# Staging, reads and rows of maxima of a two-layer attention kernel: more room and later issue

## The chip, the cores and the metric

The kernel runs on one core of a Trainium2 chip. The time is that of one execution on the device, in microseconds (us). A core has five engines that run side by side: TensorE (PE; its weight loads are listed as PEld), VectorE (DVE), ScalarE (ACT), GpSimd (POOL) and SyncE (SP), which here does nothing but issue DMAs. Each engine works through its own list of instructions in order; an instruction that waits for a semaphore holds all that stand behind it. A DMA is issued by one of the engines SP, ACT or POOL and is then carried out by 16 DMA engines. Lower times are better.

## The reference

Four sequences of 512 positions with 320 features pass two layers. A layer is self attention, cross attention to a context of 1601 positions with 192 features, and a gated feed-forward step; everything is float32, with 20 heads of 16 features.

```python
def _attn(x, ctx, wq, wk, wv, wo, bo, heads):
    q, k, v = heads_of(x @ wq), heads_of(ctx @ wk), heads_of(ctx @ wv)
    a = softmax(einsum('bhid,bhjd->bhij', q, k) * dh ** -0.5)
    return merge(einsum('bhij,bhjd->bhid', a, v)) @ wo + bo
for each layer:
    h1 = _ln(x, n1_g, n1_b);  x = _attn(h1, h1, q1, k1, v1, o1_w, o1_b, 20) + x
    h2 = _ln(x, n2_g, n2_b);  x = _attn(h2, context, q2, k2, v2, o2_w, o2_b, 20) + x
    h3 = _ln(x, n3_g, n3_b);  a, g = split(h3 @ ff_w1 + ff_b1)
    x = (a * gelu(g)) @ ff_w2 + ff_b2 + x
```

## The kernel before

**Units and chunks.** The work is cut into units. An attention unit is one sequence (b, of 4) and one group of four heads (g, of 5), so a layer has 20 units of self attention, 20 of cross attention and 4 of feed-forward. They are numbered through: layer 0 has units 0 to 19 (self), 20 to 39 (cross), 40 to 43 (feed-forward), layer 1 has 44 to 63, 64 to 83 and 84 to 87. A unit goes over its keys in chunks of 128: four chunks in self attention, 13 in cross attention. For each chunk `main` forms four score tiles (tile `st`, L1165), ScalarE takes their exponential (`pr`, L1175), and a chunk later TensorE multiplies by the values (`av`, L1189).

**High and low parts.** The products take their operands in the type float32r. Queries and keys are therefore split by `split` on GpSimd into a rounded `high` part and the rest, `low`, and a head's parts are stacked on the 32 rows of its slot: the keys as high and low, the queries once as high and low and once the other way round, so that two products sum all four terms. To bring parts to their rows they go through DRAM: writes to `qway` and `kway`, then reads into `q` and `kT`, the tiles that TensorE uses. `move` (L721) records each such group of DMAs in a queue of its unit and `carry` (L666) issues them.

**Maxima first.** The softmax subtracts the maximum of each row before the exponential. So each unit's scores are computed once before, in coarse products (`sps`, L972), and VectorE takes their maxima (`nmax` in self attention, `pm` in cross attention, L989). These products are called pairs; they are handed out by `give` beside the score products of the units before, eight of them in self attention, 26 in cross attention. `max_end` then turns the negative maxima into rows (`turned`, by a transpose on VectorE) and four small DMAs carry them to `nrows`; the third product of each score tile adds them (`st<-nrows,ones`). `max_end` of the next unit is called after the third last chunk of the current one.

**Who sets the order.** All is written out once, in Python, in program order; each engine then runs its part as semaphores allow. A counter `clock["round"]` is raised twice a chunk. Chains of smaller steps (projections `proj` and `early`, `values`, `norm`, `context`, `project`, `divide`) wait with costs and due rounds, and `steps` picks from them once a chunk. At its end it calls `carry`, which goes over the units that have moves left: a move is issued if its buffers are free and at least two rounds have passed since the unit's last move was issued or recorded, up to a budget of three DMAs a call; then come the `errands`, a queue of single tasks with a round each. In this way nearly all DMAs stand on SP's queue in the order in which `carry` met them.

**What the change touches.** `both` (L759) projects queries and keys of a self unit in two halves, into the staging tiles `low` and `high` (L718, one of each); `queries` (L795) does so for cross attention; `keys_of_context` (L823) projects the context's keys into tiles of their own, and its four writes `kway<-stages` and three reads `kT<-kway` follow. `way_free` (L747) says whether a new projection may start. `at_hand` (L1401) says whether a unit's pairs may be handed out: three rounds after its last read was issued. `add_finish` (L1052) divides a finished unit's output by its sums and writes it to `oway`; after the fifth group it adds an errand that reads the sequence's output back into `aT`, and eight `project` steps (L1094) multiply by the output weights. At the start, unit 0 is moved at once by `at_once` (L1405).

Of the kernel before, what the change touches and what calls it, by code (L numbers as in the profile page):

```python
# [9 lines left out]
F32 = mybir.dt.float32  # L10
# [7 lines left out]
B, N, D = 4, 512, 320  # L18
# [5 lines left out]
P = 128  # L24
# [41 lines left out]
def kernel(ctx: ExitStack, tc: tile.TileContext, x, context, ws, out):  # L66
# [57 lines left out]
    nc.vector.memset(fill, 1.0)  # L124


    room = {"turn": 0}

    def take_rooms(l):

# [535 lines left out]
    def carry():  # L666

        room = 3
        for _, what, u in sorted(movers):
            todo = u.moves[what]  # L670
            while todo and todo[0][1]() and clock["round"] >= u.moving[what] + 2 and room > 0:
                room -= todo[0][2]
                todo.popleft()[0]()
            if not todo:
                movers.remove((u.i, what, u))
        while errands and room > 0 and clock["round"] >= errands[0][0] and errands[0][1]():
            errands.popleft()[2]()
# [4 lines left out]
    def split(low, high):  # L682

        nc.gpsimd.tensor_copy(high.bitcast(F32R), low)
        nc.gpsimd.tensor_tensor(low, low, high, ALU.subtract)

    def add_proj(u):
# [28 lines left out]
                add(chain, 0.0, hold, due - 4, yes, lambda: "h" in u.own)  # L716

        def staged():  # L718
            return (one.tile([P, N], F32, tag=n, name=n) for n in ("low", "high"))

        def move(of, n, pairs, may=None):  # L721

            def f():
                if may is None:
                    pending[of] -= 1
                u.moving[of] = clock["round"]
                for i, (to, src) in enumerate(pairs()):
                    queue = (nc.sync, nc.scalar, nc.gpsimd)[i % 3] if start["on"] and u.i == 0 else nc.sync
                    queue.dma_start(out=to, in_=src)  # L729
                if may is not None:  # L730
                    u.open -= 1
                    if not u.open:
                        u.when = -9 if start["on"] else clock["round"]

            if may is None:
                pending[of] += 1
            u.moves[of].append((f, may or yes, n))
            u.moving[of] = clock["round"]
            if (u.i, of, u) not in movers:
                movers.append((u.i, of, u))  # L740
# [5 lines left out]

        def way_free(what):  # L747

            return not pending[what] and (len(users[what]) < 2 or not any(users[what][-2].moves.values()))

        def read_queries(t, keys=None):

# [6 lines left out]
        def both(part):  # L759

            w = N // 2
            at = part * w
            ps = step_bank([P, 512], "qkps")
            for k, _, n in DK:
                nc.tensor.matmul(  # L765
                    ps[:, :w],
                    lhsT=wqk[:n, k, u.g].rearrange("p i d -> p (i d)"),
                    rhs=first.hT[:n, k, at : at + w],
                    start=(k == 0),
                    stop=(k == 2),  # L770
                )
            if part == 0:
                u.stage = tuple(staged())
            low, high = u.stage
            if u.i == 0:
                nc.scalar.activation(high[:, at : at + w].bitcast(F32R), ps[:, :w], AF.Copy, scale=scales[:, 0:1])
                nc.vector.scalar_tensor_tensor(
                    low[:, at : at + w], ps[:, :w], scales[:, 0:1], high[:, at : at + w], ALU.mult, ALU.subtract
                )
            else:  # L780
                nc.scalar.activation(low[:, at : at + w], ps[:, :w], AF.Copy, scale=scales[:, 0:1])  # L781
            if part == 0:
                return
            if u.i:
                split(low, high)
            to_k = on_way("k").rearrange("j h d i n -> j h d (i n)")[:, :, :, :N]
            to_q = on_way("q")
            move("q", 2, lambda: [(to_k[:, 0], high[GD:]), (to_k[:, 1], low[GD:])])
            move("q", 3, lambda: [(to_q[:, e], t[:GD]) for e, t in enumerate((high, low, high))])
            read_queries(to_q, to_k)  # L790
            u.keyed = True
            first.made["q"] += 1
            first.made["k"] += 1
# [242 lines left out]
    def max_end(u):  # L1036

        parts = two.tile([P, SLOT], F32, tag="parts", name="parts")
        high, low = (parts.rearrange("p (j e t) -> p e j t", e=2, t=NQ)[:, e] for e in range(2))
        of = u.nm.rearrange("p (j t) -> p j t", t=NQ)  # L1040
        nc.vector.tensor_copy(high.bitcast(F32R), of)
        nc.vector.tensor_tensor(low, of, high, ALU.subtract)
        turned = two.tile([P, SLOT], F32, tag="turned", name="turned")

        nc.vector.transpose(turned, parts)
        slots = u.rows.bitcast(F32).rearrange("(g s) n -> s g n", s=DH)[0].rearrange("g (t r) -> g t r", t=NQ)
        for i in range(P // SLOT):
            rows = slice(i * SLOT, (i + 1) * SLOT)
            queue = (nc.sync, nc.scalar, nc.gpsimd, nc.sync)[i] if start["on"] else nc.sync
            queue.dma_start(out=slots[:, :, rows], in_=turned[rows, :])  # L1050

    def add_finish(u):  # L1052

        when = [clock["round"]]

        def since(i, n):
            return lambda: len(when) > i and clock["round"] >= when[i] + n

        turned = one.tile([P, N // SLOT, SLOT], F32, tag="oturn", name="oturn")

        def sums():
            nc.vector.transpose(turned.rearrange("p b s -> p (b s)"), u.o)
            u.rd = two.tile([P, N // SLOT], F32, tag="rd", name="rd")
            nc.vector.reciprocal(u.rd, turned[:, :, DH])
            when.append(clock["round"])

        def divide():
            nc.vector.tensor_tensor(  # L1070
                turned[:, :, :DH], turned[:, :, :DH],
                u.rd.rearrange("p (b o) -> p b o", o=1).to_broadcast([P, N // SLOT, DH]), ALU.mult,
            )
            nc.vector.transpose(u.o, turned.rearrange("p b s -> p (b s)"))
            when.append(clock["round"])

        def turn():

            way = o_way[u.b % 2]
            dma(out=way[u.g * HG : (u.g + 1) * HG].rearrange("j s n -> (j s) n"), in_=u.o)  # L1080
            if u.g < G - 1:
                return
            held["written"] += 1

            def read():
                held["read"] += 1
                aT = two.tile([P, 3, N], F32, tag="aT", name="aT")
                for k, at, n in DK:
                    dma(out=aT[:n, k, :], in_=way[at // DH : (at + n) // DH, :DH, :])
                end(aT)  # L1090

            errands.append((clock["round"] + 2, lambda: held["open"] < 2, read))

        def project(aT, t, part):  # L1094
            cols = slice(part * D // 2, (part + 1) * D // 2)
            ps = step_bank([P, 512], "ops")
            for k, at, n in DK:
                for f, m in tiles_of(P):
                    nc.tensor.matmul(  # L1099
                        ps[f : f + m, : D // 2],  # L1100
                        lhsT=aT[:n, k, t * P + f : t * P + f + m],
                        rhs=wo[:n, k, cols],
                        start=(k == 0),
                        stop=(k == 2),
                    )
            nc.vector.tensor_tensor(xs[u.b][:, t, cols], ps[:, : D // 2], xs[u.b][:, t, cols], ALU.add)

        def end(aT):
            now = clock["round"]
            held["open"] += 1  # L1110
            for t in range(NQ):
                for part in range(2):
                    add(
                        "project", (0.317,) * 3, lambda t=t, part=part: project(aT, t, part),
                        now + 6 + u.nch * t + u.nch // 2 * part, yes, lambda: clock["round"] >= now + 3,
                    )
            add("project", 0.0, done, now + 6 + u.nch * NQ)

        def done():
            held["open"] -= 1  # L1120
            after(u)

        r = when[0]
        add("divide", LIGHT, sums, r - 20, yes, since(0, 3))
        add("divide", LIGHT, divide, r - 20, yes, since(1, 1))

        add("divide", 0.0, turn, r - 20, lambda: u.g or held["written"] < held["read"] + 2, since(2, 1))


# [270 lines left out]

    def at_hand(v):  # L1401

        return v.when is not None and clock["round"] >= v.when + 3

    def at_once(v):  # L1405
        chain = "early" if v.early else "proj"
# [157 lines left out]
```

## Time and profile before

| | us |
|---|---|
| median of 3 runs | 3381.98 |
| lowest and highest | 3379.53, 3386.66 |
| profiled execution | 3384.97 |
| its span, first to last instruction | 3383.2 |
| self attention, layer 0 and layer 1 (first score to the next stage) | 443, 397 |
| cross attention, layer 0 and layer 1 | 954, 944 |
| feed-forward, layer 0 and layer 1 | 308, 283 |

The stages are cut at 55, 498, 1452, 1760, 2157 and 3101 us of the span, where the first score product of a stage starts. In a row of the waits stand who waited, for whom, the total in us, the number of waits and the longest one. In a row of the time line stand start, duration, engine (with q for its issuing part), line, operation, tiles, shapes and count, and in brackets the idle time before it and what ended it. In a row by stretches stand, for each engine, busy time and instructions, then the granted clock of TensorE, the share of the 16 DMA engines that was busy, and GB/s.

### The profile page before, as it was taken

The numbers are of one execution on the slowest core, as the hardware profiler recorded it, in microseconds if no ns is written. First come the engines' busy times: TensorE is split into PE (matmuls) and PEld (weight loads), VectorE is DVE, ScalarE is ACT, GpSimd is POOL, SyncE is SP. The second block draws the span as 40 slices with busy tenths as digits, with TensorE's granted clock in tenths as the row PEclk, the third lists the DMA queues.
The fourth block names the chain that finished last, engine by engine and source line by source line (L and its number), as shares of the span: only waits on it lengthen the run. The fifth ranks groups of instructions, "written<-read, shape, count | busy, mean of one in ns | idle before, by whom it ended". The sixth has DMA issues, their size and how long they took to land.

```text
span 3383.2 us, 81116 instructions
## 1 busy us (share of the span) xinstructions
PE 3121.4 (92%) x34290; PEld 1649.8 (49%) x34290; DVE 2096.4 (62%) x2819; ACT 1965.6 (58%) x3909; POOL 1130.3 (33%) x1224
## 2 busy tenths in 40 slices
PE   6889889999989989999999888899999899899999
PEld 3445445445545545445554554454454454454555
DVE  3657776767866876732237777667677677675221
ACT  1555656677767777830116665567677677686110
POOL 2333323443434443410113332234344344343000
PEclk7888999999989999999999999899999899999999
DMA  3343322222222222110023332222222122122000
GB/s 90 107 128 123 104 70 80 82 90 63 74 82 64 89 75 64 50 57 1 18 62 120 117 104 88 83 67 72 72 77 77 51 87 72 51 66 77 8 8 16
DMA packets 209045, 244.14 MB, mean 72 GB/s; under 512 B 60412, under 2 KB 140424, under 8 KB 208680
## 3 DMA queue, kind: packets, MB, share of 16 engines
q1 hardware_dynamic: 207924, 238.02, 22.7%
q8 instruction: 269, 4.41, 0.5%
q14 instruction: 96, 0.79, 0.1%
q10 hardware_dynamic: 308, 0.53, 0.1%
q0 software_dynamic: 448, 0.40, 0.0%
HBM read 130.03 MB, written 107.55 MB: 70 GB/s over the span
## 4 chain that ended last, share of the span: by engine, by line
PE 61%; DMA 17%; DVE 8%; SPq 5%; issue 3%; ACT 3%; POOL 1%; ACTq 0%; POOLq 0%; DVEq 0%
PE st L1165 16%; PE av L1189 13%; PE fps L1295 8%; PE yps L1349 5%; DMA q<-qway 4%; DMA qway<-low 4%; DVE pm L989 4%; DMA qway<-high 3%; PE kps L831 3%; SPq L729 3%; PE sps L972 3%; PE ops L1099 3%; ACT pr L1175 2%; DMA aT<-oway 2%; PE fps L1308 2%
## 5 line engine op out<-in xcount | busy, mean ns | idle before, releaser
L1175 ACT ACTIVATE pr<-st 128x512 f32<-128x512 f32 (+1 forms) x2720 | 1407.0, 602 | 449.5 <-PE st L1165 391.0
L989 DVE TENSOR_REDUCE pm<-sps 128x2 f32<-128x1024 f32 (+1 forms) x975 | 1135.5, 1200 | 228.3 <-PE sps L972 192.7
L1206 POOL TENSOR_TENSOR o<-o,vo 128x512 f32<-128x512 f32 x576 | 741.6, 1288 | 1431.3 <-ACT vo L1205 1412.6
L1165 PE MATMUL st<-q,kT 32*128 32x512 f32 (+1 forms) x5120 | 973.8, 448 | 32.6 <-ACT low L781 16.4
L972 PE MATMUL sps<-kT,q 32*128 32x512 f32 x4800 | 883.2, 453 | 97.8 <-DMA q<-qway 75.2
L1189 PE MATMUL av<-pr,vals 128*32 128x512 f32 (+1 forms) x5440 | 774.4, 638 | 27.4 <-ACT pr L1175 21.3
L1165 PEld LDWEIGHTS st<-q,kT 32*128 32x128 f32 (+1 forms) x5120 | 479.0, 186 | 527.4 <-ACT pr L1175 283.3
L1165 PE MATMUL st<-nrows,ones 32*128 32x512 f32 (+1 forms) x2720 | 646.4, 409 | 40.3 <-DMA nrows<-turned 40.2
L989 DVE TENSOR_REDUCE nmax<-sps 128x2 f32<-128x1024 f32 (+1 forms) x343 | 380.1, 1145 | 232.6 <-PE sps L972 179.7
L972 PEld LDWEIGHTS sps<-kT,q 32*128 32x128 f32 x4800 | 386.9, 192 | 152.8 <-DMA q<-qway 45.7
L1205 ACT COPY vo<-av 128x512 f32<-128x512 f32 x576 | 346.9, 602 | 103.7 <-PE av L1189 96.6
L1165 PEld LDWEIGHTS st<-nrows,ones 32*128 32x128 f32 (+1 forms) x2720 | 335.2, 189 | 79.5 <-DMA nrows<-turned 39.2
L1295 PE MATMUL fps<-hT,w 128*128 128x512 f32 x640 | 284.3, 597 | 0.5 <-DVE hid L1319 0.5
L1318 ACT ACTIVATE gl<-fps,b 128x512 f32<-128x512 f32 x80 | 50.7, 684 | 378.0 <-PE fps L1308 272.1
L1189 PEld LDWEIGHTS av<-pr,vals 128*32 128x32 f32 (+1 forms) x5440 | 112.7, 110 | 294.5 <-ACT pr L1175 274.5
L1319 DVE SCALAR_TENSOR_TENSOR hid<-fps,b,gl 128x512 f32<-128x512 f32 x80 | 56.4, 746 | 265.1 <-ACT gl L1318 265.1
L1295 PEld LDWEIGHTS fps<-hT,w 128*128 128x128 f32 x640 | 118.9, 190 | 148.7 <-issue 144.1
L1349 PE MATMUL yps<-w,hid 128*128 128x320 f32 x640 | 175.9, 434 | 0.4 <-ACT hT L529 0.4
L1099 PE MATMUL ops<-wo,aT 112*32 112x160 f32 (+1 forms) x3072 | 139.1, 320 | 27.7 <-DMA aT<-oway 27.4
L1099 PEld LDWEIGHTS ops<-wo,aT 112*32 112x32 f32 (+1 forms) x3072 | 101.3, 118 | 112.7 <-issue 50.7
L1349 PEld LDWEIGHTS yps<-w,hid 128*128 128x128 f32 x640 | 120.5, 190 | 55.7 <-issue 6.6
L781 ACT ACTIVATE low<-qkps,scales 128x256 f32<-128x256 f32 x78 | 35.3, 473 | 157.4 <-PE qkps L765 70.6
(92 smaller groups left out, 2532.5 us busy)
## 6 DMA issues: line engine op xcount, KB each, us to landing
kway<-stages SPq DMA_DIRECT2D x160, 224.0 KB
q<-qway SPq DMA_DIRECT2D x138, 256.0 KB
kT<-kway SPq DMA_DIRECT2D x80, 384.0 KB
oway<-o SPq DMA_DIRECT2D x80, 256.0 KB
kT<-kway SPq DMA_DIRECT2D x40, 256.0 KB
qway<-high SPq DMA_DIRECT2D x160, 64.0 KB
qway<-high SPq DMA_DIRECT2D x79, 128.0 KB
aT<-oway SPq DMA_DIRECT2D x32, 224.0 KB
```

Source lines behind the costliest of these rows:

```text
L729: queue.dma_start(out=to, in_=src)
L831: nc.tensor.matmul(ps[i * GD : (i + 1) * GD, :w], lhsT=wk_q[rows, k, u.g * GD : (u.g + 1) * GD], rhs=first.kvT[rows, k, i * HALF : i * HAL ...
L972: nc.tensor.matmul(ps, lhsT=u.q[j * SLOT : (j + 1) * SLOT, e, t * P : (t + 1) * P], rhs=u.kT[j * SLOT : (j + 1) * SLOT, u.k0 + s * 512 : u ...
L989: nc.vector.tensor_reduce(to[:, j : j + n], part, AX.X, ALU.max, negate=(ns == 1))
L1099: nc.tensor.matmul(ps[f : f + m, : D // 2], lhsT=aT[:n, k, t * P + f : t * P + f + m], rhs=wo[:n, k, cols], start=(k == 0), stop=(k == 2),)
L1165: nc.tensor.matmul(st[:r, :], lhsT=ones[rows, :r] if e == 2 else u.keys(rows, c), rhs=u.rows[rows, :] if e == 2 else u.q[rows, e, :], star ...
L1175: nc.scalar.activation(p[:r], st[:r], AF.Exp)
L1189: nc.tensor.matmul(ps[j * SLOT : (j + 1) * SLOT, :], lhsT=columns_of[:r, head : head + SLOT], rhs=pr.pop((c, j))[:r, :], start=True, stop= ...
L1205: nc.scalar.copy(vo, ps)
L1206: nc.gpsimd.tensor_tensor(u.o, u.o, vo, ALU.add)
L1295: nc.tensor.matmul(ps, lhsT=w1[:, k, i * FF + c * P : i * FF + (c + 1) * P], rhs=u.hT[:, k, :], start=ahead and k == 0, stop=not ahead and ...
L1349: nc.tensor.matmul(ps[:, :D], lhsT=hid[c][:, t * P : (t + 1) * P], rhs=w2[:, c, :], start=(c == 0), stop=(c == NHC - 1),)
```

## The change

- **Two sets of staging tiles, one output tile.** `low` and `high` come from the pool with two buffers, `aT` from the one with one buffer. `way_free` no longer refuses a projection of queries while writes of an earlier unit are still to be issued; for the context's keys it still does. The output's read now waits until no projection of an earlier output is open.
- **First unit's parts go straight to their rows.** Unit 0 isn't written to DRAM: 24 DMAs, one for each head, half and place, copy 16 rows each from `high` and `low` to `q` and `kT`, on SP, ACT and POOL in turn.
- **Rows of maxima in cross attention are issued a chunk later.** Where a unit and the one before it are both cross attention, the four DMAs of `max_end` become an errand for the next round, put ahead of the other errands; `carry` comes to it after the moves.
- **Reads spaced.** In `carry` a read needs three rounds since the last move, a write still two. Pairs are at hand four rounds after the read instead of three. The output's read comes four rounds after its write instead of two, and its projection five rounds after the read instead of three.

```diff
-            while todo and todo[0][1]() and clock["round"] >= u.moving[what] + 2 and room > 0:
+            while todo and todo[0][1]() and clock["round"] >= u.moving[what] + 3 - todo[0][3] and room > 0:
...
-            return (one.tile([P, N], F32, tag=n, name=n) for n in ("low", "high"))
+            return (two.tile([P, N], F32, tag=n, name=n) for n in ("low", "high"))
...
-            u.moves[of].append((f, may or yes, n))
+            u.moves[of].append((f, may or yes, n, may is None))
...
-            return not pending[what] and (len(users[what]) < 2 or not any(users[what][-2].moves.values()))
+            return not (what == "k" and pending[what]) and (len(users[what]) < 2 or not any(users[what][-2].moves.values()))
...
+            if u.i == 0:
+                for j in range(HG):
+                    for t in range(2):
+                        for h in range(2):
+                            of = (high, low)[h]
+                            slot = slice(j * SLOT + h * DH, j * SLOT + (h + 1) * DH)
+                            away = slice(j * SLOT + (1 - h) * DH, j * SLOT + (2 - h) * DH)
+                            rows = slice(j * DH + t * GD, j * DH + t * GD + DH)
+                            to = [u.kT[slot, u.k0 : u.k0 + N]] if t else [u.q[slot, 0, :], u.q[away, 1, :]]
+                            for x in to:
+                                queue = (nc.sync, nc.scalar, nc.gpsimd)[room["first"] % 3]
+                                room["first"] += 1
+                                queue.dma_start(out=x.bitcast(F32), in_=of[rows, :])
+                u.when = -9
+                u.keyed = True
+                first.made["q"] += 1
+                first.made["k"] += 1
+                return
...
-        for i in range(P // SLOT):
-            rows = slice(i * SLOT, (i + 1) * SLOT)
-            queue = (nc.sync, nc.scalar, nc.gpsimd, nc.sync)[i] if start["on"] else nc.sync
-            queue.dma_start(out=slots[:, :, rows], in_=turned[rows, :])
+
+        def rows():
+            for i in range(P // SLOT):
+                part = slice(i * SLOT, (i + 1) * SLOT)
+                queue = (nc.sync, nc.scalar, nc.gpsimd, nc.sync)[i] if start["on"] else nc.sync
+                queue.dma_start(out=slots[:, :, part], in_=turned[part, :])
+
+        if u.cross and u.before.cross:
+            errands.appendleft((clock["round"] + 1, yes, rows))
+        else:
+            rows()
...
-                aT = two.tile([P, 3, N], F32, tag="aT", name="aT")
+                aT = one.tile([P, 3, N], F32, tag="aT", name="aT")
...
-            errands.append((clock["round"] + 2, lambda: held["open"] < 2, read))
+            errands.append((clock["round"] + 4, lambda: held["open"] < 1, read))
...
-                        now + 6 + u.nch * t + u.nch // 2 * part, yes, lambda: clock["round"] >= now + 3,
+                        now + 6 + u.nch * t + u.nch // 2 * part, yes, lambda: clock["round"] >= now + 5,
...
-        return v.when is not None and clock["round"] >= v.when + 3
+        return v.when is not None and clock["round"] >= v.when + 4
```

2 lines of the change are left out of this document (1 added, 1 removed).

## The prediction

> **What bounds the kernel now.** I read the page first, for the engine that carries the time; then its busy time by stage; then what TensorE waited for; last SyncE's own order in time, because every wait found leads to a DMA issued there.
>
> ```profile
> PE 3121.4 (92%) x34290; PEld 1649.8 (49%) x34290; DVE 2096.4 (62%) x2819; ACT 1965.6 (58%) x3909; POOL 1130.3 (33%) x1224
> PE   6889889999989989999999888899999899899999
> PEclk7888999999989999999999999899999899999999
> ```
>
> ```profile
> core 0: 3383.2 us, clock 0.946
> ```
>
> TensorE is busy for 92% and idle for 3383.2 - 3121.4 = 262 us. The clock row says that it also ran at a mean of 0.946; if the lower clock is one half, that is 2 x 0.054 x 3383 = 365 us at half speed and at most 183 us of work lost to it. Idle plus slow clock is all that this change can touch. By stage (self and cross of layer 0, then of layer 1):
>
> ```profile
> core 0: us, PE busy (x) PEld busy (x) DVE busy (x) ACT busy (x) POOL busy (x), PEclk, DMA share, GB/s
> 55.00:498.00 443.00, 380.98 (x4186) 209.11 (x4182) 292.61 (x438) 240.06 (x482) 140.27 (x170) 0.88 0.33 106
> 498.00:1452.00 954.00, 889.01 (x11702) 461.05 (x11699) 685.77 (x838) 700.93 (x1407) 392.76 (x369) 0.95 0.25 76
> 1760.00:2157.00 397.00, 346.19 (x4100) 192.99 (x4098) 283.82 (x404) 234.14 (x472) 130.76 (x149) 0.93 0.32 104
> 2157.00:3101.00 944.00, 888.54 (x11695) 457.68 (x11690) 675.60 (x796) 700.65 (x1403) 391.98 (x369) 0.95 0.24 72
> ```
>
> The two self stages idle 62 + 51 us, the two cross stages 65 + 55 us. No other engine is near full: VectorE has 66 to 72% of each stage. So waits, not work, are at stake. TensorE's waits over the whole span, and one of ScalarE's:
>
> ```profile
> PE sps L972 <- DMA q<-qway: 75.2, 30, 15.4
> PE st L1165 <- DMA nrows<-turned: 40.2, 12, 5.8
> PE st L1165 <- ACT low L781: 29.7, 12, 4.1
> PE ops L1099 <- DMA aT<-oway: 27.4, 24, 3.0
> PE sps L972 <- DMA kT<-qway: 5.8, 3, 2.6
> PE vps L896 <- ACT low L781: 3.3, 1, 3.3
> ACT low L781 <- DMA qway<-low: 60.5, 14, 6.7
> ```
>
> **The price of a microsecond of idling.** Idle time also lowers the clock. Two neighbouring units of cross attention, the first with long waits, the second with none:
>
> ```profile
> 747.00:804.30 57.30, 48.92 (x596) 25.54 (x592) 34.74 (x40) 35.04 (x72) 16.43 (x14) 0.85 0.17 54
> 804.30:851.80 47.50, 46.72 (x756) 26.56 (x752) 34.94 (x42) 35.40 (x73) 21.22 (x18) 1.00 0.24 73
> ```
>
> The first idles 8.4 us, the second 0.8 us, and it is 9.8 us longer: 1.29 per us of idling, a low value since it has fewer matmuls. The ceiling over the kernel is (262 + 183) / 262 = 1.70. I take 1.4, an estimate between the two. Short waits pay too: this stretch has one wait of 2 us and a clock of 0.79.
>
> ```profile
> 411.00:427.00 16.00, 13.27 (x120) 5.88 (x124) 11.61 (x16) 8.48 (x16) 3.23 (x4) 0.79 0.32 119
> 418.29 0.96 PE L972 MATMUL sps<-kT,q 32*128 32x512 f32 x10 [2.04 <-DMA q<-qway]
> ```
>
> [...]
>
> **The change, part by part** (in us of TensorE idling).
>
> *Two sets of staging tiles, and projections no longer held until the last writes are issued.* Today ScalarE's write of low waits until the unit before has been read out (60.5 us). Behind it in ScalarE's queue stand the exponentials, and the matmul banks that they empty: 29.7 + 3.3 = 33.0 us reach TensorE. With a second set the tile was last read a whole unit ago. Bounds 20 and 33; I take 28, since a few waits on ScalarE have other ends. What comes next there is VectorE, with its maxima (row below).
>
> *Reads a chunk after the last write, pairs at hand a chunk later.* Of 75.2 + 5.8, the start's 15.4 is another case: 65.6 us. In the issue order of the two programs, a self unit's read now follows its last write by two chunks instead of one, and its writes are often issued a chunk earlier; many cross units project queries one or two chunks earlier, because they no longer wait for pending writes, and some gain a chunk between read and use. But SP still issues in order, and where the key read stands before the query read it holds it as before. Bounds 20 and 60; I take 45, since most of these waits are 2 to 3 us and a chunk lasts 2.7 us or more. The later start bunches pairs: in the second chunk of unit 17 of either layer (and once at the start) ten pairs of maxima are issued, against two to five today.
>
> ```profile
> L989 DVE TENSOR_REDUCE nmax<-sps 128x2 f32<-128x1024 f32 (+1 forms) x343 | 380.1, 1145 | 232.6 <-PE sps L972 179.7 <-PE st L1165 51.8
> ```
>
> Eight more reductions of 1.15 us are 9 us of VectorE in a chunk of 5; the chunks around it are lighter by as much. Loss 8 over the three, bounds 0 and 20.
>
> *First unit straight to its rows.* Eight writes and reads through DRAM become 24 copies, eight on each of three queues.
>
> ```profile
> 15.46 0.66 SPq L729 DMA_DIRECT2D kway<-high  x1
> 15.94 3.30 POOL L535 TENSOR_TENSOR x<-x,brow 128x320 f32<-128x320 f32 x4 [9.52 <-DMA brow<-in_L_xattn_o_b_dram]
> 19.18 0.84 POOL L729 DMA_DIRECT2D qway<-high  x1
> 26.62 0.70 POOL L729 DMA_DIRECT2D q<-qway  x1 [6.60 <-DMA qway<-high]
> 30.37 0.80 PE L972 MATMUL sps<-kT,q 32*128 32x512 f32 x4 [15.44 <-DMA q<-qway]
> ```
>
> SP needs 8 x 0.66 = 5 us from 15.5. GpSimd is the late one: its additions end at 19.2, eight issues of 0.8 us end at 25.7, and its read of today shows about 3 us from issue to use (27.3 to 30.4): 28.7 against 30.4. Gain 2, bounds -3 and 6. ScalarE's eight issues have nothing behind them until the next unit is projected.
>
> *Output tile read, and projected two rounds later; one tile.* The eight projections now start at least two chunks after the read instead of one. Of 27.4, bounds 10 and 27; I take 20. The single tile adds a wait: the next read must wait until the eight projections are done. Batches are 20 chunks apart in self and 65 in cross, so that hides it; without this cover each batch would pay the read's landing, at least the 3.0 us of the longest such wait today.
>
> *Rows of maxima a chunk later in cross attention.* This is the part against the change. The errand runs after the movers of its round, so key writes that today stand behind the rows on SP's queue now stand before them. What that does is in today's trace, where four, two or none stand before (unit starts at 747.02, 2846.34 and 851.79):
>
> ```profile
> 737.73 5.46 SPq L729 DMA_DIRECT2D kway<-stages  x4
> 743.29 4.66 SPq L1050 DMA_DIRECT2D nrows<-turned  x4
> 747.02 0.50 PE L1165 MATMUL st<-q,kT 32*128 32x512 f32 x2
> 752.21 0.80 PE L1165 MATMUL st<-nrows,ones 32*128 32x512 f32 x2 [4.46 <-DMA nrows<-turned]
> ...
> 2838.82 2.72 SPq L729 DMA_DIRECT2D kway<-stages  x2
> 2842.12 3.72 SPq L1050 DMA_DIRECT2D nrows<-turned  x4
> 2846.34 0.49 PE L1165 MATMUL st<-q,kT 32*128 32x512 f32 x2
> 2847.69 0.50 PE L1165 MATMUL st<-nrows,ones 32*128 32x512 f32 x2 [0.61 <-DMA nrows<-turned]
> ...
> 851.13 5.47 SPq L729 DMA_DIRECT2D kway<-stages  x4
> 851.79 0.50 PE L1165 MATMUL st<-q,kT 32*128 32x512 f32 x2
> ```
>
> Rows behind four key writes are usable 752.21 - 737.73 = 14.5 us after the first of them, behind two 8.9 us; they are needed 0.75 us into the unit. The first write comes 9.3, 7.5 and 0.7 us before the start when keys are projected after the 9th, 10th and 12th chunk; for the 11th I take 4.1, midway. In the issue order of the changed kernel, nine cross units have four writes before the rows with keys after the 9th chunk (wait 14.5 - 9.3 - 0.75 = 4.45), five after the 10th (6.25), seven have two writes with keys after the 11th (4.05), and two have four a chunk earlier still (1.8, by a chunk of 2.7). That is 40.0 + 31.3 + 28.4 + 3.6 = 103 us. Today's waits of this kind in the two cross stages:
>
> ```profile
> PE st L1165 <- DMA nrows<-turned: 11.6, 3, 4.5
> PE st L1165 <- DMA nrows<-turned: 16.3, 5, 5.2
> ```
>
> So it adds 103 - 28 = 75. Bounds 20 (only the 9th-chunk units, less than today's rest) and 116 (all 23 at 6.25). In self attention the rows are not moved, but the first cross unit's keys are written earlier there: of the other 40.2 - 27.9 = 12.3, gain 7, bounds 0 and 12.
>
> **The sum.** 28 + 45 + 2 + 20 + 7 = 102 gained, 75 + 8 = 83 lost: 19 us less idling, times 1.4 is 27 us. The profiled execution took 3384.97 (span 3383.2), 3 us over the median of the runs; from the median 3381.98 it gives 3355.
>
> **The rivals.**
> *Slower.* The rows wait behind key writes longer than I priced: with other waits gone the chunks before a unit's start shorten, and the first write falls nearer to it. If all 23 units wait 6.25, the sum is 102 - 116 - 8 = -22, times 1.4: 3413. It decides from (102 - 8 + 28) / 23 = 5.3 us a unit on. For it: such waits already reach 5.2 us today, in an order that becomes the rule. Against it: longer waits at the start push the writes ahead of the next start.
> *Much faster.* The key writes drain before the rows in all but the 9th-chunk units: 40 - 28 = 12 lost, 102 - 12 - 8 = 82, times 1.4: 3267. For it: behind two writes today's wait is only 0.6 us. Against it: there the writes were issued 7.5 us ahead, which an 11th-chunk projection doesn't give.
> [...]
>
> **How the numbers follow.** Chances: the sum as worked out 0.38, its own range 3320 to 3374; much faster 0.22; slower 0.32; no change 0.08. About 0.2% (7 us) is what runs of this kernel can tell from no change, so faster is 0.38 + 0.22 = 0.60, same 0.08, slower 0.32. The range reaches to the middle case on either side and a little beyond, since both prices of the rows are estimates: 3280 to 3425.
>
> **What the changed profile would show.** Right: ScalarE's wait for qway<-low near 0 and TensorE's for low under 6 us; waits for q<-qway near 35 us (15 at the start among them); for aT under 8; waits for nrows near 110 us, with four key writes ahead of the rows on SP; self stages shorter by 30 us or more each, cross stages no shorter. Wrong: nrows under 60 us (then much faster), or over 130 (slower); waits for q unchanged; a new wait of VectorE in the self stages.

## The result, and the profile after

The changed kernel takes 3351.99 us (median of 4 runs, 3350.45 to 3355.70) beside 3383.14 us for the kernel before on the same chip: a ratio of 0.991, 95% interval 0.9892 to 0.9927. It is faster by 31 us; 27 had been forecast. In what follows, times taken beside different runs of the kernel before (3372 to 3390 us) are compared by their ratios, and "us" of a ratio are of 3383.

Two rows of the page of the changed kernel, and its clock:

```profile
PE 3113.5 (93%) x34290; PEld 1642.0 (49%) x34290; DVE 2105.4 (63%) x2841; ACT 1965.0 (59%) x3909; POOL 1131.7 (34%) x1230
PEclk7899999899998999999999999999998999999999
```

```profile
core 0: 3349.8 us, clock 0.952
```

TensorE idles 3349.8 - 3113.5 = 236 us instead of 262. By stage (self and cross attention of layer 0, then of layer 1; columns as in the prediction):

```profile
43.80:460.40 416.60, 368.69 (x4218) 202.50 (x4214) 289.02 (x442) 241.16 (x484) 141.00 (x171) 0.93 0.35 113
460.40:1433.00 972.60, 896.26 (x11662) 463.52 (x11662) 694.42 (x845) 698.82 (x1405) 391.04 (x369) 0.94 0.25 75
1741.50:2101.80 360.30, 332.77 (x4131) 183.84 (x4130) 281.04 (x402) 235.24 (x473) 131.69 (x149) 0.98 0.35 113
2101.80:3065.50 963.70, 897.36 (x11659) 463.01 (x11656) 679.50 (x807) 699.19 (x1402) 390.59 (x369) 0.94 0.23 71
```

The self stages are 26 and 37 us shorter, the cross stages 19 and 20 us longer, and the first stage starts at 43.8 us instead of 55. Two things of opposite sign, then, as forecast. The waits of TensorE name them:

```profile
PE st L1190 <- DMA nrows<-turned: 92.6, 33, 7.2
PE sps L990 <- DMA q<-qway: 37.9, 19, 5.8
PE av L1214 <- ACT pr L1200: 31.9, 130, 0.5
PE sps L990 <- DMA kT<-low: 8.8, 2, 8.6
PE vps L914 <- ACT low L781: 0.6, 1, 0.6
```

The waits for `low` (33.0) and for `aT` (27.4) are gone, those for `q` have halved (75.2), those for the rows of maxima have more than doubled (40.2). Unit 24 shows the new order on SyncE's queue, and what TensorE then did:

```profile
652.28 5.51 SPq L729 DMA_DIRECT2D kway<-stages  x4
657.89 4.46 SPq L1070 DMA_DIRECT2D nrows<-turned  x4
```

```profile
666.91 0.79 PE L1190 MATMUL st<-nrows,ones 32*128 32x512 f32 x2 [7.18 <-DMA nrows<-turned]
```

Four key writes, then the four rows, used 666.91 - 652.28 = 14.6 us after the first key write; the prediction had 14.5. In the eleven other cross units that waited over a microsecond behind four key writes it was 14.2 to 15.3 us.

The start: the first unit's products begin at 23.5 us, 6.8 us earlier than before, but right behind its first scores the second unit waits for its own reads, 5.8 us and then 2.3.

```profile
23.54 0.76 PE L990 MATMUL sps<-kT,q 32*128 32x512 f32 x1 [8.61 <-DMA kT<-low]
...
50.01 0.79 PE L990 MATMUL sps<-kT,q 32*128 32x512 f32 x2 [5.76 <-DMA q<-qway]
```

### The profile page after: what moved, and what is told of

It is laid out like the page before. It is cut to its first block, busy times and chain, and to the rows that moved or that the text cites. A ratio compares the mean times of both kernels' runs of the same rounds, so it can differ in the third digit from the quotient of the medians.

```text
span 3349.8 us, 81113 instructions
## 1 busy us (share of the span) xinstructions
PE 3113.5 (93%) x34290; PEld 1642.0 (49%) x34290; DVE 2105.4 (63%) x2841; ACT 1965.0 (59%) x3909; POOL 1131.7 (34%) x1230
## 4 chain that ended last, share of the span: by engine, by line
PE 69%; DMA 11%; DVE 9%; ACT 5%; SPq 4%; issue 2%; POOL 1%; ACTq 0%; POOLq 0%; DVEq 0%
PE st L1190 20%; PE av L1214 16%; PE fps L1320 8%; PE yps L1374 5%; DVE pm L1007 4%; DMA nrows<-turned 4%; ACT pr L1200 3%; DMA q<-qway 3%; PE sps L990 3%; PE vps L932 3%; PE kps L849 3%; PE ops L1124 2%; PE qkps L765 2%; PE fps L1333 2%; SPq L1070 2%
## 5 line engine op out<-in xcount | busy, mean ns | idle before, releaser
L1190 PE MATMUL st<-q,kT 32*128 32x512 f32 (+1 forms) x5120 | 980.2, 452 | 23.5 <-DVE pm L1007 7.2
L990 PE MATMUL sps<-kT,q 32*128 32x512 f32 x4800 | 874.2, 454 | 67.2 <-DMA q<-qway 37.9
L1214 PE MATMUL av<-pr,vals 128*32 128x512 f32 (+1 forms) x5440 | 774.6, 638 | 37.9 <-ACT pr L1200 31.9
L1190 PE MATMUL st<-nrows,ones 32*128 32x512 f32 (+1 forms) x2720 | 645.9, 414 | 92.8 <-DMA nrows<-turned 92.6
L1374 PEld LDWEIGHTS yps<-w,hid 128*128 128x128 f32 x640 | 120.5, 190 | 55.8 <-issue 6.6
L1124 PE MATMUL ops<-wo,aT 112*32 112x160 f32 (+1 forms) x3072 | 125.9, 302 | 0.9 <-DVE pm L1007 0.5
L765 PE MATMUL qkps<-hT,wqk 112*128 112x256 f32 (+1 forms) x480 | 125.0, 405 | 0.9 <-DVE hid L1344 0.9
```

Of the source, the lines that this page charges most:

```text
L765: nc.tensor.matmul(ps[:, :w], lhsT=wqk[:n, k, u.g].rearrange("p i d -> p (i d)"), rhs=first.hT[:n, k, at : at + w], start=(k == 0), stop=( ...
L990: nc.tensor.matmul(ps, lhsT=u.q[j * SLOT : (j + 1) * SLOT, e, t * P : (t + 1) * P], rhs=u.kT[j * SLOT : (j + 1) * SLOT, u.k0 + s * 512 : u ...
L1124: nc.tensor.matmul(ps[f : f + m, : D // 2], lhsT=aT[:n, k, t * P + f : t * P + f + m], rhs=wo[:n, k, cols], start=(k == 0), stop=(k == 2),)
L1190: nc.tensor.matmul(st[:r, :], lhsT=ones[rows, :r] if e == 2 else u.keys(rows, c), rhs=u.rows[rows, :] if e == 2 else u.q[rows, e, :], star ...
L1214: nc.tensor.matmul(ps[j * SLOT : (j + 1) * SLOT, :], lhsT=columns_of[:r, head : head + SLOT], rhs=pr.pop((c, j))[:r, :], start=True, stop= ...
L1374: nc.tensor.matmul(ps[:, :D], lhsT=hid[c][:, t * P : (t + 1) * P], rhs=w2[:, c, :], start=(c == 0), stop=(c == NHC - 1),)
```

## The experiments

### The part against the change: rows of maxima a chunk later

**Undone.** The changed kernel, without this part alone:

```diff
-        if u.cross and u.before.cross:
-            errands.appendleft((clock["round"] + 1, yes, rows))
-        else:
-            rows()
+        rows()
```

> The changed kernel with one part undone: the rows of maxima are issued at once in cross attention too, as before the change. My theory (the later issue puts the rows behind the key writes and costs TensorE some 65 us of idling, at 1.3 to 1.4 us each): waits for nrows fall from 92.6 us to 25 to 40, and the time to 3352 - 60 x 1.35 = about 3270 (3255 to 3290). Rival (the delay of the rows costs little; the same transfers only end elsewhere, because key writes now wait behind the rows instead): waits for kT or q grow by what nrows gives back, and the time stays at 3345 to 3355.

Measured: 3258.74 us, ratio 0.9654 (0.9632 to 0.9675). TensorE's wait for rows and the two cross stages:

```profile
PE st L1187 <- DMA nrows<-turned: 39.6, 22, 5.0
```

```profile
456.70:1390.00 933.30, 880.42 (x11658) 454.42 (x11658) 692.04 (x844) 697.83 (x1404) 391.09 (x369) 0.96 0.26 78
2061.60:2973.50 911.90, 874.92 (x11648) 451.48 (x11644) 678.98 (x806) 697.66 (x1401) 391.04 (x369) 0.98 0.24 74
```

The waits fall by 53 us and the time by 87: the cross stages shrink by 39 and 52 us, and nothing takes the waits' place. The theory holds, the rival falls. The whole change without this part would have gained 3.5% instead of 0.9%.

**Alone.** The kernel before with this part only (the same lines added).

> The kernel before with one part done alone: the rows of maxima a chunk later in cross attention. My theory: waits for nrows go from 40.2 us to 100 or more, nothing else changes, and the time is 3383 + 65 x 1.35 = about 3470 (3440 to 3500). Rival (with the staging waits still there, a chunk of delay is hidden by them): 3383, at most 3400.

Measured: 3449.41 us, ratio 1.0215 (1.019 to 1.0241).

```profile
PE st L1172 <- DMA nrows<-turned: 83.6, 22, 6.5
PE sps L972 <- DMA q<-qway: 74.5, 29, 15.6
PE st L1172 <- ACT low L781: 28.9, 11, 4.1
PE ops L1106 <- DMA aT<-oway: 23.3, 24, 2.2
```

The other waits stay as they were and hide little of it: 73 us lost here, 87 in the changed kernel. The waits rose less than I expected (83.6, not 100).

**Late, but first in their round.** The rows are still issued a chunk later, but by a queue of their own at the head of `carry`, before the moves.

```diff
+    ripe = deque()
...
     def carry():
+        while ripe and clock["round"] >= ripe[0][0]:
+            ripe.popleft()[1]()
...
-            errands.appendleft((clock["round"] + 1, yes, rows))
+            ripe.append((clock["round"] + 1, rows))
```

> The changed kernel; the rows are still issued a chunk later in cross attention, but at the head of their round, ahead of the reads and writes of queries and keys that fall due in it. Theory A (the place behind the key writes costs, not the delay itself): waits for nrows fall below 45 us and the time comes to 3260 to 3295. Theory B (the chunk of delay itself costs, since the rows are then wanted at once): waits for nrows stay at 70 us or more and the time at 3330 to 3355. Where the delay alone moves them past writes of an earlier round, a time between the two.

Measured: 3264.96 us, ratio 0.967 (0.9651 to 0.9689), the same as with the rows at once (0.9654) within the intervals. Unit 24 again (SyncE's queue), and the wait over the whole span:

```profile
651.27 2.75 SPq L732 DMA_DIRECT2D kway<-stages  x2
654.13 4.14 SPq L1073 DMA_DIRECT2D nrows<-turned  x4
658.32 1.14 SPq L732 DMA_DIRECT2D kway<-stages  x2
```

```profile
PE st L1193 <- DMA nrows<-turned: 41.9, 25, 4.8
```

Two key writes stand ahead instead of four, and the unit takes 44.5 us instead of 52.5. So the delay costs nothing that the intervals can tell; the place behind the key writes costs the rest (theory A).

**On another queue.** Late and behind the moves as in the changed kernel, but issued by ScalarE: `queue = nc.scalar` for these rows.

> The changed kernel; the rows are still issued a chunk later in cross attention, but on ScalarE's queue instead of SyncE's. Theory A (the cost is the order in SyncE's queue, where the rows' issues wait until SyncE has issued the key writes): waits for nrows fall below 45 us, time 3270 to 3300, with 4 x 0.05 to 4 x 0.7 us of issuing on ScalarE a unit. Theory B (the cost is in the transfers: the key writes occupy the same DMA engines that the rows need, whatever queue they are issued from): waits for nrows stay at 70 us or more and the time at 3340 to 3360.

Measured: 3454.94 us, ratio 1.0231 (1.0202 to 1.0259), worse than either theory had it. ScalarE's time line at unit 25's end, its wait, and TensorE's:

```profile
757.69 0.61 ACTq L1072 DMA_DIRECT2D nrows<-turned  x1
...
758.34 2.00 ACTq L1072 DMA_DIRECT2D nrows<-turned  x3
760.39 2.05 ACT L1202 ACTIVATE pr<-st 65x512 f32<-65x512 f32 x4 [2.34 <-DMA nrows<-turned]
```

```profile
ACT pr L1202 <- DMA nrows<-turned: 90.0, 29, 8.3
```

```profile
PE av L1216 <- ACT pr L1202: 130.6, 176, 7.2
PE st L1192 <- DMA nrows<-turned: 47.8, 25, 4.5
```

The exponentials stand behind four issues of 0.6 us each on ScalarE, and TensorE waits 131 us for them instead of 32. The shorter wait for rows (47.8) is thus no proof for theory A: TensorE was waiting already. What speaks for theory B is the landing. A unit's rows are 128 packets of 128 bytes in the trace. In cross attention, rows with no key write in the 12 us ahead of them have, in most units, all landed 3.2 to 3.7 us after their first issue; with four ahead, 4.0 to 8.1 us in the changed kernel, where SyncE issues them (8.0 in unit 24), and 6.6 to 10.0 us here, where SyncE does not. Clearer still are six units of this run with no key write ahead: SyncE's first one came 1.6 us after the rows' first issue, ScalarE had started all four by 2.1 us, as in units without key writes, and still the rows landed after 7.3 to 7.6 us. So in these units the key writes held the rows up after their issue, though another queue had issued them. In seven more units both queues issued at once, and the rows landed after 10.7 to 13.6 us; there their own fourth issue came late too (4.8 to 8.3 us after the first), so issuing is not free of it. That the two meet on the same DMA engines, as theory B has it, is an inference from these landings; which engine carried which packet is not shown. Nor was the issuing cheap here: the rows' 153 issues on ScalarE took 124 us in all, and none took less than 0.595 us; the 0.05 us of the expectation is shown by no run.

### Each of the other parts

From here on the kernel with the rows at once (0.9654) is the base, and one further part of the change is undone.

**One staging set, and projections held** (`low` and `high` from the pool with one buffer, `way_free` as before, so this undoes two things at once).

> The kernel with the rows of maxima issued at once (3259 us), with one more part undone: one set of staging tiles, and projections held until the last writes are issued. My theory (a second set takes ScalarE's wait for qway<-low away, worth 28 to 33 us of TensorE's idling): TensorE's waits for low come back to 25 to 33 us, time 3259 + 28 x 1.35 = about 3297 (3285 to 3310). Rival (with the reads spaced, the tile is read out earlier too, and one set would do): waits for low under 10 us, time 3255 to 3270.

Measured: 3392.10 us, ratio 1.0048 (1.0032 to 1.0064): 133 us lost, where 38 were expected, and with few waits for `low` (11.9 + 7.9 us). The loss lies in the self stages (481 and 419 us to the next stage's start, against 413 and 363 in the base). Its longest chunk, in unit 14, takes 24 us; a second, in unit 16, takes 15:

```profile
377.20:401.20 24.00, 14.20 (x82) 7.61 (x82) 5.80 (x8) 4.53 (x10) 3.75 (x4) 0.65 0.26 90
438.90:454.20 15.30, 12.40 (x79) 5.56 (x77) 14.31 (x19) 3.21 (x7) 1.89 (x2) 0.73 0.11 37
```

```profile
379.17 0.84 ACT L781 ACTIVATE low<-qkps,scales 128x256 f32<-128x256 f32 x2 [3.95 <-DMA qway<-low]
392.66 0.84 ACT L781 ACTIVATE low<-qkps,scales 128x256 f32<-128x256 f32 x2 [7.89 <-DMA qway<-low]
```

In the first, a projection's two halves each wait for the tile to be written out, and the wait for the reads follows in the same chunk; in the second VectorE is busy for 14.31 of 15.30 us with maxima that have come all at once. My reading is that one set with spaced reads delays the projections until the pairs are due. It is seen in these two chunks, which take 39 us together where a median chunk of the base takes 4.3; the self stages lost 124 us, and their median chunk rose to 5.2, so the loss is not these two's alone.

**Reads close again** (a read two rounds after the last move, pairs at hand after three).

> The kernel with the rows of maxima issued at once (3259 us), with the spacing undone: reads may follow the last write after two chunks counted as before, and pairs are at hand a chunk earlier, as before the change. My theory (the spacing is worth about 45 us of TensorE's waits for q): waits for q<-qway and kT<-qway rise from 34 to 65 us or more, time 3259 + 32 x 1.35 = about 3302 (3285 to 3325). Rival (these waits went because the projections, no longer held, come earlier, not because of the spacing): waits for q stay at 30 to 45 us, time 3255 to 3275.

Measured: 3242.69 us, ratio 0.9612 (0.9591 to 0.9632). Faster, by 14 us (give or take some 10), where the theory had it slower by 43.

```profile
PE sps L990 <- DMA q<-qway: 32.1, 16, 6.5
...
PE sps L990 <- DMA kT<-qway: 7.6, 3, 3.8
```

The waits for `q` do not come back: 32.1 us, against 33.6 with spaced reads; those for `kT<-qway` are 7.6 against 0.6. The spacing did not take them away. The chunk of unit 4 in which ten pairs of maxima were bunched takes 8.4 instead of 17.2 us, that of unit 17 4.3 instead of 11.7 (unit 4, first the base, then reads close):

```profile
142.60:159.80 17.20, 14.99 (x101) 7.93 (x97) 9.93 (x14) 4.82 (x10) 5.34 (x14) 0.79 0.32 117
148.10:156.50 8.40, 7.47 (x56) 4.40 (x53) 6.51 (x9) 4.41 (x9) 2.47 (x7) 1.00 0.33 100
```

But the self stages as a whole are not shorter for it: 421 and 361 us, against 413 and 363 in the base. What is shorter are the two cross stages, 924 and 897 us against 933 and 912, mostly by the clock: TensorE idles there 9 us less in all and is at half clock for 34 us less.

```profile
464.10:1388.30 924.20, 873.14 (x11710) 455.57 (x11706) 688.29 (x840) 699.66 (x1407) 390.00 (x368) 0.97 0.26 79
2053.90:2950.50 896.60, 866.44 (x11704) 452.95 (x11700) 677.25 (x798) 698.16 (x1403) 389.89 (x368) 0.98 0.24 75
```

So the bunching is real, but the 14 us are not shown to be its price; what close reads gain in the cross stages stays open.

**Half of the spacing** (reads still spaced, pairs at hand after three rounds).

> The kernel with the rows at once (3259 us), with half of the spacing undone: reads still follow the last write a chunk later, but pairs are at hand after three counted chunks again instead of four. Undoing both halves gave 3243. Theory A (the later hand-over is what costs: pairs wait a chunk longer than their data and are then bunched on VectorE, chunks of 17.2 and 11.7 us): 3240 to 3248, and waits for q about as many as with both undone. Theory B (the later reads themselves cost, as they land later): 3255 to 3262. Theory C (late reads used early collide): waits for q over 45 us, time over 3265.

Measured: 3267.76 us, ratio 0.9637 (0.9621 to 0.9654), between the two and not separable from the base. Waits for `q` rose to 45.9 us: reads that start later, used as early as before, are waited for, as theory C said, but the time isn't over the base. Which half costs more stays open.

**Both, one set and close reads**, which closes the square.

> The kernel with the rows at once (3259 us), with both the second staging set and the spacing of the reads undone; with the runs of each alone (one set 3392, close reads 3243) it makes a square of four. Theory A (spaced reads and one set hold each other up: the projection waits for reads that wait a chunk more, the pairs of maxima come late and in bunches, so most of the 133 us that one set cost is not there with close reads): self stages of 440 and 394 us as in the kernel before, against 410 and 360, time 3243 + 64 = about 3310 (3295 to 3325). Theory B (the second set is worth 133 us by itself): 3243 + 133 = about 3375.

Measured: 3284.27 us, ratio 0.9686 (0.9669 to 0.9703).

| | reads close | reads spaced |
|---|---|---|
| one staging set | 0.9686 | 1.0048 |
| two staging sets | 0.9612 | 0.9654 |

With close reads the second set is worth 25 us, with spaced reads 133. Spacing costs 14 us with two sets and 122 with one. This is theory A, with the second set worth even less than its 64 us; how the two hold each other up was seen in the two chunks above only. The lower left number has a second message: one set and close reads leave only the output's part and the first unit of the whole change, and that is 106 us faster than the kernel before.

**The output read after two rounds and projected from the third** (still one tile).

> The kernel with the rows of maxima issued at once (3259 us), with the output's rounds undone: the output tile is read two rounds after its write and projected from the third, as before the change; its tile stays single. My theory: waits for aT come back to 20 to 27 us, time 3259 + 24 x 1.35 = about 3291 (3280 to 3300). Rival (the waits were short, and the projections only move the work that fills the others): waits for aT under 10 us, or replaced by as much less of others, time 3255 to 3268.

Measured: 3299.25 us, ratio 0.9772 (0.9756 to 0.9789): 40 us lost, near the theory's number but not by its way. The waits for `aT` are 5.6 us, not 20 to 27; the rest of the 23 us more of idling is spread over rows (+5), the output's additions on VectorE (`x`, +6) and others. I could not assign it.

**The output's part alone**, on the kernel before.

```diff
-                aT = two.tile([P, 3, N], F32, tag="aT", name="aT")
+                aT = one.tile([P, 3, N], F32, tag="aT", name="aT")
...
-            errands.append((clock["round"] + 2, lambda: held["open"] < 2, read))
+            errands.append((clock["round"] + 4, lambda: held["open"] < 1, read))
...
-                        now + 6 + u.nch * t + u.nch // 2 * part, yes, lambda: clock["round"] >= now + 3,
+                        now + 6 + u.nch * t + u.nch // 2 * part, yes, lambda: clock["round"] >= now + 5,
```

> The kernel before with one part done alone: one output tile, read four rounds after its write and projected from the fifth. Together with the first unit's direct copies (worth 11 us elsewhere) this part brought the kernel before from 3390 to 3284, far more than the 28 us that its waits for aT (27.4 us) would give. Theory A (the output's early reads also stand in SyncE's queue ahead of queries' reads, and waited there for their data): waits for aT fall to 10 us or less, waits for q<-qway from 75.2 to 45 to 52 us, time about 0.972 of before (0.967 to 0.977). Theory B (the first unit's copies are worth more beside one staging set, because they shift the start of every later move): waits for q stay at 60 us or more, time 0.980 to 0.990 of before.

Measured: 3281.13 us, ratio 0.9729 (0.9703 to 0.9755): 92 us from this part alone, as theory A had it.

```profile
PE sps L972 <- DMA q<-qway: 50.6, 21, 15.1
...
PE ops L1099 <- DMA aT<-oway: 6.6, 12, 0.8
```

It takes 21 us from the waits for `aT`, 25 from those for `q` and 15 from those for `low` (29.7 to 14.7), which the prediction had given to the staging. How, is best seen in cross unit 79 of the kernel before and of this one (the whole unit; then waits of the kernel before inside it, and three stretches of 3.4 us around them; last the whole unit with the part):

```profile
2888.50:2945.40 56.90, 48.03 (x600) 25.05 (x596) 34.65 (x40) 35.04 (x72) 16.53 (x14) 0.88 0.18 55
```

```profile
2924.49 0.65 PE L1099 MATMUL ops<-wo,aT 112*32 112x160 f32 x8 [2.32 <-DMA aT<-oway]
2925.96 0.76 PE L1099 MATMUL ops<-wo,aT 112*32 112x160 f32 x8 [0.81 <-DMA aT<-oway]
2927.24 0.76 PE L1099 MATMUL ops<-wo,aT 96*32 96x160 f32 x8 [0.52 <-DMA aT<-oway]
```

```profile
2921.80:2925.20 3.40, 1.03 (x12) 0.19 (x8) 0.69 (x1) 1.08 (x3) 1.26 (x1) 0.92 0.28 103
2925.20:2928.60 3.40, 2.12 (x24) 0.98 (x28) 0.32 (x1) 0.00 (x0) 0.00 (x0) 0.50 0.07 28
2928.60:2932.00 3.40, 3.40 (x36) 1.52 (x32) 2.45 (x2) 2.06 (x4) 0.00 (x0) 0.58 0.00 0
```

```profile
2790.50:2837.50 47.00, 44.93 (x692) 24.79 (x688) 34.65 (x41) 35.01 (x74) 18.07 (x16) 1.00 0.22 70
```

After three short waits in a row the clock is at about half for two stretches, and ScalarE and VectorE have little work at first. In this unit, waits for rows fall from 4.7 to 0.6 us as well (two key writes stand ahead of them instead of four), and it is 10 us shorter; of this, the outputs' share is not separated. Six outputs are read inside the self stages. In the kernel before, query writes stood close behind the output's read on SyncE's queue in all six (2.4 to 4.3 us later); with the part, in one: that is theory A's mechanism. But the waits for `q` fell most in the cross stages (21.7 to 9.3 and 11.7 to 5.1 us), where the order around that read is the same in both. There only the shift of all later moves can be seen (in units 25, 69, 74 and 79 the next key writes come 25 to 26 us after the output's read instead of 36 to 37), and what causes it is not shown.

**The first unit through DRAM again.**

> The kernel with the rows of maxima issued at once (3259 us), with the first unit's parts through DRAM again, as before the change. My theory by the changed kernel's trace (the first unit's products start 7 us earlier, but the second unit then waits 6 to 8 us for its own reads): the start is worth 0 to 7 us, waits at the start longer by about 7 us, time 3259 to 3269. Rival (the start of cross attention's first unit in time comes 11 us earlier with the direct copies, all of it lasting): 3270 to 3275.

Measured: 3270.40 us, ratio 0.9688 (0.9673 to 0.9703): the direct copies are worth about 11 us, give or take some 9, so rather the rival's number, though both fit.

### A version that gains more

In the faster kernel with close reads, five cross units (25, 30, 35, 69, 74) wait most for their rows, with four key writes still ahead of them. Here such writes wait, in chunks 8 to 10, until the rows are out:

```diff
+    held = {"open": 0, "written": 0, "read": 0, "rows": False}
...
+            if held["rows"] and u.cross and todo and todo[0][3]:
+                continue
...
+            held["rows"] = u.cross and not last and u.nch - 5 <= c < u.nch - 2
...
                 max_end(nxt)
+                held["rows"] = False
```

> The kernel with the rows at once and close reads (3243 us); in addition, key writes that fall due in chunks 8 to 10 of a cross unit wait until that unit's next rows of maxima are issued. Five units still have four key writes ahead of their rows and wait 3.3 to 5.2 us for them (22.8 us in all). Theory (the key writes' transfers delay the rows): these five waits go, nrows falls from 38 to 18 us or less, time 3243 - 20 x 1.35 = about 3216 (3205 to 3228). Rival (the writes held come late for their own reads, or hold the queries' moves up): new waits for kT or q of 10 us and more, time 3235 to 3260.

Measured: 3237.36 us, ratio 0.9552 (0.9535 to 0.9569), 20 us better by ratio than without it; the best version here.

```profile
PE ops L1123 <- DMA aT<-oway: 20.3, 17, 3.5
PE st L1189 <- DMA nrows<-turned: 11.4, 7, 3.1
...
PE sps L992 <- DMA kT<-qway: 10.4, 4, 4.2
```

The waits for rows fall to 11.4 us, as the theory had it, and in the cross stages none is left; some of the gain is given back to `aT` (20.3 us against 3.3), and 20 us were gained where 27 were expected.

## Why the prediction was right, and which of its steps were not

The sum came out 4 us from the measurement, but by errors that cancel: that it came so near is luck. One path from the kernel before to the changed one, each step between two measured ratios (each good to some 8 us):

| step | ratio after it | measured us | the prediction's term x 1.4 |
|---|---|---|---|
| output tile read and projected later | 0.9729 | -92 | -28 |
| first unit direct | 0.9686 | -15 | -3 |
| second staging set, projections not held | 0.9612 | -25 | -39 |
| reads spaced | 0.9654 | +14 | -52 (with the loss of 8) |
| rows a chunk later | 0.9910 | +87 | +95 (with the gain of 7 in self) |
| sum | | -31 | -27 |

- **Rows a chunk later** was right in mechanism and place. The rule "behind four key writes 14.5 us after the first" holds in this run (14.2 to 15.3 us). The classes came out as priced where the first write fell as assumed: seven units behind two writes wait 4.0 us on average (priced 4.05), four with keys after the 10th chunk 6.2 (6.25). But eight with keys after the 9th (nine had been forecast) waited only 2.0 to 3.5 us and not 4.45, since their first key write came 10.6 to 11.9 us before the start and not 9.3. So the cross stages wait 76 us for rows and not 103, and the gain of 7 in self attention did not come (16.6 us against 12.4). That the time fits, 87 us against 95, is the price's doing: 56 us of idling (180 to 236) cost 1.6 each, not 1.4.
- **Reads spaced** was the failed step. "65.6 us, I take 45" booked waits to the edit that seems made for them. The waits for `q` did fall to 37.9 us, near the 35 forecast, but the output's later read took 25 us of them, the first unit's copies some 17, and undoing the spacing brings none back. The match is luck in itself: after the start, 55.8 us fell to 29.8, where 20 were forecast, and at the start 8.1 are left where 15 were, with 8.8 more for `kT<-low`. In place of 52 us gained, the spacing lost 14. Its bunched maxima are there, but the self stages are no longer for them; the loss lies in the cross stages, and its cause is open.
- **Output later** was mis-sized threefold. "27.4, I take 20" counted the waits on one row of the list and took the clock at 1.4; alone, the part cut 59 us of idling (262 to 203, between profiled executions of two sessions), 40 of them in waits for `q` and `low`, and was worth 92 us.
- **Staging** was right that the waits for `low` go (33.0 to 0.6), but half of those for `low` had gone with the output's part, and the set is worth 25 us with close reads and 133 with spaced ones: the term depended on the next one, and the sum treated them as independent.
- **First unit** gained 11 to 15 us, not 3: the products begin at 23.5 us and not at 28.7, since GpSimd's eight issues took 0.5 us each, not 0.8, and the first product came 0.5 us after the last of them, not 3. The longer wait of the second unit (5.8 us, 1.0 before) takes back less than the earlier start brings.
- **The rivals.** Slower (all 23 units at 6.25 us) fell with the rows' waits at 92.6. Much faster fell too, but its time, 3267, is nearly that of the kernel with the rows at once. No change fell with the time.
- **Of the signs**, the self stages were to be shorter by 30 us or more each: layer 0's is so by 26 only.

## What to carry to other kernels

A row of the waits tells who stood still, not what an edit is worth: 27 us of waits for one tile were worth 92, and of 66 us of waits for another about half went, with edits not aimed at them. When several parts of a change move one in-order DMA queue, measure each alone and undone before believing a sum, and two by two where one delays what the other needs. Issue small DMAs that the next stage needs at once ahead of large ones that have time; the place in the queue was worth 81 to 87 us here, a whole chunk of delay nothing that could be told.

## What the runs showed of the hardware

**The clock falls after short waits too, and its loss is a matter of how often.** In all these traces TensorE's granted clock is full or one half, and it stays at half for mostly a multiple of 3.41 us (51 of 52 times in the kernel before, 44 of 45 in the changed one), 7.0 us on average in the kernel before. It fell 52 times there (365 us at half clock), 45 times in the changed kernel (323 us), 34 with the rows at once (217 us, at a mean clock of 0.967) and 28 with reads close besides (184 us, 0.972). Those last two kernels idle alike, 180 and 184 us; the second is 14 us faster by ratio (24 between the profiled spans), and 33 us less at half clock are 16 us of work. Cut into stretches of 3.41 us, the one ahead of a fall had a median of 2.0 us of idling in the kernel before, and in none of the traces did a stretch with more than 2.0 us pass without a fall (at full clock there were 27 such stretches in the kernel before, 26 in the changed one). The reverse does not hold: 2 to 12 falls of an execution followed a stretch with less than 1 us of idling, which this does not explain. Idling for a part of a stretch was enough here: the one from 2921.80 above is busy for 1.03 of 3.40 us, and the next has a clock of 0.50.

**Idling has no fixed price.** From before to after, 33 us of span went with 25.5 us of idling, 1.3 each. One staging set with spaced reads and two sets with close reads, profiled in one session on one chip, differ by 35 us of idling (219 and 184) and by 157 us of span (3391.5 and 3234.7), 4.5 each. Half of the 170 us more at half clock explains 85 of the 157; with the idling that leaves 37 open. The prediction's 1.4 is near the first; its ceiling of 1.70, an average over one kernel, was no ceiling.

**ScalarE pays for the DMAs it issues.** Four issues, 0.6 us each in the median and up to 2.2, ahead of the exponentials cost it 90 us over 29 waits, and the kernel 3.2% against the same rows on SyncE.
